# Queries of a cross-attention by seven products over pairs of batches, 256 columns a matmul, on one core

## The chip, the cores and the metric

The kernel runs on one core of a Trainium2 chip, in float32. The metric is the device time of one execution in microseconds; the kernel before took 573.75 us (median of three runs, 572.99 to 574.35).

## The reference

```python
def _L0_xattn_ref(hidden_states, memory_keys, memory_values, attention_mask, Wq, Wout, ln_gamma, ln_beta):
    residual = hidden_states                      # (8, 256, 1024)
    mu = jnp.mean(hidden_states, axis=-1, keepdims=True)
    var = jnp.var(hidden_states, axis=-1, keepdims=True)
    x = (hidden_states - mu) * jax.lax.rsqrt(var + LN_EPS) * ln_gamma + ln_beta
    Q = _split_heads(x @ Wq.T)                    # 32 heads of 32
    K = _split_heads(memory_keys)
    V = _split_heads(memory_values)
    scores = jnp.einsum('bhsd,bhtd->bhst', Q, K) * HEAD_DIM ** (-0.5)
    scores = jnp.where(attention_mask[:, None, None, :], scores, -jnp.inf)
    probs = jax.nn.softmax(scores, axis=-1)
    attn = jnp.einsum('bhst,bhtd->bhsd', probs, V)
    attn = attn.transpose(0, 2, 1, 3).reshape(B, S, HIDDEN)
    return residual + attn @ Wout.T
```

Keys and values are the same array, the context, of 256 rows for each of the 8 batches.

## The kernel before

The work is a software pipeline over 64 steps n. A step is a batch (n // 8) and a group of four heads (n % 8), that is 128 of the 1024 query features. Iteration n of the loop issues, for different steps, everything that is due: the scores of step n+1 on TensorE (`sc`, four PSUM banks, one set only), pieces of the output projection of the batch before (`po`), the values of earlier steps (`pv`), the query matmuls that are due (`pq`, one bank), and then the softmax of step n+1. The softmax goes over all engines: VectorE subtracts and masks (`e<-sc`, with the row minimum `mn` beside it), ScalarE takes the exponential and its sum (`e<-e,mn`), VectorE the reciprocal (`rden`), GpSimd or, for heads listed in the plan, ScalarE normalises (`e<-e,rden`), VectorE transposes in blocks of 32 (`pT<-e`), and DMAs on SP's queue swap the blocks (`pT<-pT`, `pT<-pc`). Since there is one set of four `sc` banks, the scores of the next step wait until VectorE has read all of this one's.

The order within each engine is written by hand: the calls in an iteration, and the table `PLAN`, which says in which iteration each side job is issued. An entry of `wq`, for example, is [iteration, name, quarter, engine]; the numbers under `b2`, `b3`, `rel` (after: `b2`, `b3`, `even`, `odd`) are the iterations of the loads, statistics, normalisations, transposes (`xe<-x`) and block moves (`xnT<-xe`, DMAs) of a batch's x. `qp` names DMAs that go to GpSimd's queue; all others go to SP's.

Side jobs that matter here: the normalisation of x needs `bn_stats`, an `rstd` on GpSimd, a `shift` on GpSimd and one ScalarE instruction for each half of 128 rows. The output projection is done by seven products instead of eight, with sums of `wo` on GpSimd (`wo<-wo`) and sums of the attention output `at`, and its results are added into `r`. `make_q` computes a group's queries plainly, with eight matmuls of 256 columns. For batches from `SPLIT` = 3 on, the queries are computed by seven products too (`query_product`): one batch's two halves of 128 rows are the two block rows, the features the block columns. Each product has 16 matmuls of 128 columns, written into `pq`; sums of weights (`sum_wq`) are made in place of weights that are not needed any more, sums of x (`sum_x`) go into a buffer `sx`, the weights that three of the products take are kept in DRAM and loaded again for each batch into `ring` (`load_ring`), and `copy_product` carries results from PSUM to `qa`. A float32 matmul appears as two records in the trace. Products stand in iterations 8(b-1)+2 to 8(b-1)+8: 18 to 24, 26 to 32, and so on to 50 to 56.

## Time and profile before

| what | value |
|---|---|
| runs | 572.99, 573.75, 574.35 us |
| profiled execution, span from first to last instruction | 572.0 us |
| median of the runs less that span | 1.75 us |
| mean granted TensorE clock | 1.000 |
| TensorE matmul busy | 562.9 us (98%) |
| weight loads, beside the matmuls | 394.6 us (69%) |
| VectorE busy | 466.2 us (81%) |
| ScalarE busy | 450.5 us (79%) |
| GpSimd busy | 399.1 us (70%) |
| DMA, SP's and GpSimd's queue, share of 16 engines | 55.2% and 15.1% |

The profile gives for the profiled execution its span; its own time as a run isn't given beside it. In the timeline a row is start, duration, engine, line, operation, output and inputs, with the number of instructions, and in square brackets the idle time before it and what ended it. In a group row the two numbers behind the bar are the busy time and the mean ns of one instruction. Names are shown without the buffer number, so `sc` is any of the score banks.

### The profile page before, as it was taken

To read this page: it belongs to the slowest core of one execution; us is meant where nothing else is said; L and a number is where in the kernel's file an instruction comes from. 1 tells how busy PE (TensorE), PEld (TensorE's weight loads), DVE (VectorE), ACT (ScalarE), POOL (GpSimd) and SP (SyncE) were. 2 spreads that over 40 slices of the span, in tenths; PEclk is the share of its full clock that TensorE was granted. 3 is DMA by queue.
4 is the path that set the end of the run, shared out by engine and by line. 5 is a ranking of instruction groups with operands and counts; after the bars stand their busy time and mean duration, and the time that the engine had idled before them with its cause. 6 is when DMAs were issued, how large, how long until landed. Compare 5 with 4: busy or idle time off the path is not lost.

```text
span 572.0 us, 20001 instructions
## 1 busy us (share of the span) xinstructions
PE 562.9 (98%) x7162; PEld 394.6 (69%) x7162; DVE 466.2 (81%) x1701; ACT 450.5 (79%) x1527; POOL 399.1 (70%) x643
## 2 busy tenths in 40 slices
PE   8999999999999999999999999999999999999998
PEld 7788775767667677667675777667766777755454
DVE  5988899988878888988788987898877878688833
ACT  3699978888779877888768988789868888879920
POOL 1478978887678895787667774686955875267690
PEclk9999999999999999999999999999999999999999
DMA  8768778576777677877888677767866765547551
GB/s 298 278 174 252 203 206 230 133 205 189 203 235 203 205 207 220 257 210 205 214 249 234 206 201 221 229 200 209 233 189 193 226 182 175 145 136 228 153 167 74
DMA packets 45891, 116.93 MB, mean 204 GB/s; under 512 B 9136, under 2 KB 9904, under 8 KB 45792
## 3 DMA queue, kind: packets, MB, share of 16 engines
q1 hardware_dynamic: 38080, 90.14, 55.2%
q0 software_dynamic: 7424, 25.50, 15.1%
q8 instruction: 57, 0.93, 0.7%
q14 instruction: 42, 0.34, 0.2%
q10 hardware_dynamic: 288, 0.01, 0.0%
HBM read 64.23 MB, written 11.53 MB: 132 GB/s over the span
## 4 chain that ended last, share of the span: by engine, by line
PE 69%; DVE 9%; POOL 8%; ACT 6%; issue 4%; DMA 3%; SPq 0%; DVEq 0%; ACTq 0%; POOLq 0%
PE po_S L930 17%; PE pq_A L615 16%; PE sc L654 8%; PE pv L840 8%; PE po_A L930 8%; PE pq_S L615 6%; POOL e L714 5%; ACT e L698 3%; DVE e L694 3%; PE po_end L997 3%; DVE pT L720 3%; DMA pT<-pT 2%; ACT e L712 1%; PE pq L513 1%; DMA wq<-in_wq_dram 1%
## 5 line engine op out<-in xcount | busy, mean ns | idle before, releaser
L698 ACT ACTIVATE e<-e,mn 128x256 f32<-128x256 f32 x512 | 253.7, 502 | 32.8 <-DVE mn L694 30.2
L714 POOL TENSOR_SCALAR e<-e,rden 128x256 f32<-128x256 f32 x408 | 188.5, 476 | 125.0 <-DVE rden L708 116.8
L720 DVE STREAM_TRANSPOSE pT<-e 128x512 f32<-128x512 f32 x256 | 180.4, 707 | 54.6 <-POOL e L714 23.5
L694 DVE CUSTOM_DVE_ANT_0 e<-sc,mb 128x256 f32<-128x256 f32 x512 | 185.1, 415 | 13.0 <-PE sc L654 12.0
L726 ACT COPY pc<-pT 128x512 f32<-128x512 f32 x128 | 78.8, 617 | 43.7 <-DVE pT L720 28.5
L698 ACT ACTIVATION_READ_ACCUMULATOR e<-e,mn 128x1 f32 x512 | 98.9, 193 | 0.0
L513 PE MATMUL pq<-xnT,wq 128*128 128x256 f32 (+1 forms) x368 | 84.5, 383 | 0.0
L513 PEld LDWEIGHTS pq<-xnT,wq 128*128 128x128 f32 x368 | 68.6, 190 | 14.6 <-issue 3.4
L930 PE MATMUL po_S<-wo,at 128*128 128x512 f32 x152 | 73.5, 606 | 1.0 <-DVE r L972 0.7
L654 PE MATMUL sc<-k,qa 32*128 32x256 f32 x1024 | 73.8, 401 | 0.1
L654 PEld LDWEIGHTS sc<-k,qa 32*128 32x128 f32 x1024 | 45.9, 184 | 39.0 <-issue 17.8
L840 PE MATMUL pv<-pT,v_all 64*32 64x128 f32 x3584 | 61.0, 273 | 1.0 <-ACT e L712 0.6
L840 PEld LDWEIGHTS pv<-pT,v_all 64*32 64x32 f32 x3584 | 51.9, 105 | 12.8 <-issue 7.7
L930 PE MATMUL po_A<-wo,at 128*128 128x512 f32 x128 | 59.3, 604 | 0.1
L930 PE MATMUL po_S<-wo,s 128*128 128x512 f32 x104 | 49.9, 607 | 0.3 <-DVE rden L708 0.3
L708 DVE RECIPROCAL rden<-den 128x2 f32<-128x2 f32 x256 | 37.9, 148 | 13.1 <-ACT e L698 12.1
L712 ACT ACTIVATE e<-e,rden 128x256 f32<-128x256 f32 x104 | 46.8, 500 | 1.0 <-DVE rden L708 1.0
L615 PEld LDWEIGHTS pq_A<-xnT,wq 128*128 128x128 f32 x352 | 41.1, 192 | 5.6 <-issue 4.7
L930 PEld LDWEIGHTS po_S<-wo,at 128*128 128x128 f32 x152 | 26.0, 190 | 25.7 <-issue 23.9
L694 DVE DVE_READ_ACCUMULATOR2_ANT mn<- 128x1 f32 x512 | 42.3, 83 | 0.0
L615 PE MATMUL pq_A<-xnT,wq 128*128 128x128 f32 x352 | 41.2, 275 | 0.3 <-issue 0.3
L930 PEld LDWEIGHTS po_A<-wo,at 128*128 128x128 f32 x128 | 23.0, 189 | 26.5 <-issue 24.4
(116 smaller groups left out, 687.6 us busy)
## 6 DMA issues: line engine op xcount, KB each, us to landing
pT<-pT SPq DMA_DIRECT2D x128, 128.0 KB, 3.4
pT<-pc SPq DMA_DIRECT2D x128, 128.0 KB, 4.0
v_all<-in_kv_dram POOLq DMA_DIRECT2D x17, 512.0 KB, 4.8
k<-in_kv_dram SPq DMA_DIRECT2D x30, 256.0 KB, 4.2
r<-in_x_dram SPq DMA_DIRECT2D x26, 256.0 KB, 4.0
ring<-kept_T SPq DMA_DIRECT2D x11, 512.0 KB, 5.8
xnT<-xe SPq DMA_DIRECT2D x79, 64.0 KB, 3.9
out_dram<-r POOLq DMA_DIRECT2D x18, 256.0 KB, 3.7
```

Source lines behind the costliest of these rows:

```text
L513: nc.tensor.matmul(pqs[n], wq[:, o, c, :], xnTs[b](c), start=(c == 0), stop=(c == NC - 1),)
L615: nc.tensor.matmul(pqs[b][:, o, :], w[:, c], x_[:, c], start=begins and o + c == 0, stop=c == NK - 1, skip_group_check=True,)
L654: nc.tensor.matmul(scs[n][j][:, s, :], qa[r, n % NQ, ts(s, P)], ks[n - n % 2][r, n % 2, :], start=True, stop=True,)
L694: nc.vector.tensor_tensor_reduce(out=e[:, s, :], in0=pss[j][:, s, :], in1=mbs[n // NQ], scale=1.0, scalar=NO_SCORE, op0=ALU.add, op1=ALU.m ...
L698: nc.scalar.activation(e[:, s, :], e[:, s, :], AF.Exp, bias=mn[:, s : s + 1], scale=-1.0, accum_out=den[:, s : s + 1],)
L708: nc.vector.reciprocal(rden, dens[j])
L712: engine.activation(es[j][:, s, :], es[j][:, s, :], AF.Copy, scale=rden[:, s : s + 1])
L714: engine.tensor_scalar(es[j][:, s, :], es[j][:, s, :], rden[:, s : s + 1], 1.0, ALU.mult, ALU.mult,)
L720: nc.vector.transpose(pT[:, :, :, j, :, :].rearrange("p a i s k -> p (a i) s k"), es[j].rearrange("p s (b t) -> p b s t", t=K),)
L726: nc.scalar.copy(pc[:, :, ts(j, 2)], pT[:, 1, :, ts(j, 2)])
L840: nc.tensor.matmul(pvs[n][r][j * HD : (j + 1) * HD], vs[n - n % 2][ts(r, 2 * K), n % 2, i, ts(j, HD)], pT[ts(r, 2 * K), :, i, j, :, :], st ...
L930: nc.tensor.matmul(po, operand(b, name)[:, c], wo[:, which, c], start=begins and c == 0, stop=c == NK - 1, skip_group_check=not begins,)
```

## The change

Two batches at a time, (2,3), (4,5) and (6,7), become the two block rows of the seven products, so `SPLIT` is 2 and batch 2 is included. A product is done in two halves of two 128-feature groups, each with 8 matmuls of 256 columns (all rows of one batch); there are 14 half products for a pair, in iterations 8b-6 to 8b+7 for even b: 10 to 23, 26 to 39 and 42 to 55. The sums of x are written in place over `xnT` (24 GpSimd instructions instead of 20). The odd batch's queries lie in `qlo` and `qhi` (the latter in the first half of `ring`), from which `scores` reads them. ScalarE copies three of the products with 36 instructions of 256 columns (before 80 of 128), VectorE adds the others with 24 instructions (before 15), and GpSimd adds `qlo` to `qhi` after P6 (`after`). The sums of weights take other places and other forms, all on GpSimd, at iterations 7 to 20 (before, 3 of 16 on VectorE, 11 to 22). Weights B11, B21, T1 and half of T3 are kept and loaded again in 14 loads (before 26). The preparation of x is rescheduled in pairs: batch 3's loads move to iterations 5 and 6, its statistics to 7 and 8, its normalisations to 8 and 9 and both transposes to 9. The plan of the output projection (`aside`, `p1late`) now treats batches 0, 2 and 4 in one way and the others in the other. The entries of `qp` for `ring` and most `mv` DMAs are gone, so that these are issued on SP's queue: GpSimd's DMA instructions fall from 75 to 53.

```diff
-PLAN = {'wq': [[14, 'T1', 3, 'V'], [17, 'T3', 0, 'P'], [11, 'T1', 0, 'P'], ...
+PLAN = {'wq': [[7, 'T1', 0, 'P'], [7, 'T1', 1, 'P'], [10, 'T2', 0, 'P'], ...
...
- 'b3': {'loads': [-13, -11],
-        'stats': [-10, -9],
-        'norms': [-9, -8],
-        'trans': [-8, -6],
+ 'b3': {'loads': [5, 6],
+        'stats': [7, 8],
+        'norms': [8, 9],
+        'trans': [9, 9],
...
- 'SPLIT': 3,
- 'rings': [[-3, -3], [0, 0], [2, 2]],
+ 'SPLIT': 2,
+ 'rings': {'B11': [-8, -6], 'B21': [-7, -5], 'T1': [-4, -2], 'T3': [None, 1]},
...
+ 'aside': [0, 2, 4],
...
- 'p1late': [0, 3, 2, 4, 5],
+ 'p1late': [0, 2, 4],
...
+    PRODUCTS_Q = (
+        ("P1", 0), ("P2", 0), ("P1", 1), ("P2", 1), ("P5", 0), ("P6", 0), ("P3", 0),
+        ("P5", 1), ("P6", 1), ("P3", 1), ("P7", 0), ("P4", 0), ("P7", 1), ("P4", 1),
+    )
+    FACTORS = {
+        "P1": ("A11", "B11"), "P2": ("A12", "B21"), "P3": ("S4", "B22"), "P4": ("A22", "T4"),
+        "P5": ("S1", "T1"), "P6": ("S2", "T2"), "P7": ("S3", "T3"),
+    }
...
     def query_product(b, p):
-        name, which, begins = Q_PRODUCTS[p]
...
-            pqs[b] = ps_q.tile([P, NK, P], F32, tag="pq", name=f"pq_{b}_{name}")
...
-        for o in range(NK):
-            w = weights(which, o)
+        name, half = PRODUCTS_Q[p]
+        begins = name not in ("P2", "P4")
+            pqs[b] = ps_q.tile([P, 2, S], F32, tag="pq", name=f"pq_{b}_{name}")
+        x_, w_ = FACTORS[name]
+        x_, w = x_part(b, x_), weights_of(b, w_, half)
+        for o in range(2):
             for c in range(NK):
                 nc.tensor.matmul(
-                    pqs[b][:, o, :], w[:, c], x_[:, c], start=begins and o + c == 0,
-                    stop=c == NK - 1, skip_group_check=True,
+                    pqs[b][:, o, :], w[:, o, c], x_[:, :, c].rearrange("p a s k -> p s a k"),
+                    start=begins and o + c == 0, stop=c == NK - 1, skip_group_check=True,
                 )
...
+        to, of = {
+            "P6": (qlo, qlo), "P3": (c12, qhi), "P7": (qhi, qhi), "P4": (qlo, qlo),
+        }[name]
+        nc.vector.tensor_tensor(to if name == "P3" else to[:, two], pqs[b], of[:, two], ALU.add)
+        if name == "P6":
+            after.append(partial(nc.gpsimd.tensor_tensor, qhi[:, two], qhi[:, two], qlo[:, two], ALU.add))
...
+    def query(n):
+
+        b, o = divmod(n, NQ)
+        if b < 2 or b % 2 == 0:
+            return qa[:, o]
+        return qlo[:, o] if o < NK else qhi[:, o - NK]
...
-    firsts = {NQ * (b - 1) + 2: b for b in range(SPLIT, B)}
-    products = {n + p: (b, p) for n, b in firsts.items() for p in range(len(Q_PRODUCTS))}
+    PAIRED = range(SPLIT, B, 2)
+    products = {NQ * b - 6 + p: (b, p) for b in PAIRED for p in range(len(PRODUCTS_Q))}
```

Three places show how the instructions stand. The first is GpSimd between the normalisation of step 8 (`e_2`, `e_3`) and that of step 9 (`e_0` behind it), first before, then after:

```order
L714 TENSOR_SCALAR e_2_1299<-e_2_1299,rden_2_1323 128x256 x2
L714 TENSOR_SCALAR e_3_1310<-e_3_1310,rden_3_1329 128x256 x2
L534 TENSOR_TENSOR wq<-wq,gs 128x1024
L350 TENSOR_TENSOR wo<-wo 128x512
L714 TENSOR_SCALAR e_0_1418<-e_0_1418,rden_0_1441 128x256 x2
```

The names in the rows after are the same, with other buffer numbers.

```order
L709 TENSOR_SCALAR e_2_1301<-e_2_1301,rden_2_1329 128x256 x2
L709 TENSOR_SCALAR e_3_1312<-e_3_1312,rden_3_1336 128x256 x2
L394 TENSOR_TENSOR rstd_1325<-ve_0_1341,mhalf 128x1
L515 TENSOR_TENSOR wq<-wq,gs 128x1024
L337 TENSOR_TENSOR wo<-wo 128x512
L560 TENSOR_TENSOR ring<-wq 128x512 x2
L709 TENSOR_SCALAR e_0_1430<-e_0_1430,rden_0_1453 128x256 x2
```

An `rstd` of batch 3 and two sums T1 (`ring<-wq`) have come in ahead of step 9's normalisation.

The second is VectorE between the block transposes of step 10 and the first read of step 11's scores (`e_0<-sc_0`), before:

```order
L708 RECIPROCAL rden_3_1593<-den_3_1575 128x2
L720 STREAM_TRANSPOSE pT_1544<-e_2_1562 128x8x64
L720 STREAM_TRANSPOSE pT_1544<-e_3_1573 128x8x64
L399 BN_STATS st_1_1609<-x_1158 128x6 x2
L402 BN_AGGR mv_1456<-st_1_1609 128x2
L404 TENSOR_SCALAR ve_1_1613<-mv_1456 128x1
L694 ISA e_0_1645,mn_0_1646<-sc_0_1622,mb_1215 128x256
```

And after, where `xe` is the transposed x of batch 3:

```order
L703 RECIPROCAL rden_3_1608<-den_3_1590 128x2
L715 STREAM_TRANSPOSE pT_1559<-e_2_1577 128x8x64
L715 STREAM_TRANSPOSE pT_1559<-e_3_1588 128x8x64
L471 STREAM_TRANSPOSE xe_1627<-x_1159 128x32x32 x2
L689 ISA e_0_1661,mn_0_1662<-sc_0_1638,mb_1216 128x256
```

The statistics of the second half of x_3 went to an earlier step, and both transposes of x_3 came to this one, behind ScalarE's normalisation of that half.

The third is TensorE between the scores of step 25 (the first two rows) and those of step 26 (the last two), before:

```order
L654 MATMUL sc_2_3507<-k_3040,qa 128x256
L654 MATMUL sc_3_3508<-k_3040,qa 128x256
L930 MATMUL po_S_3320<-wo,at_1_2329 128x512 x2
L615 MATMUL pq_A_3519<-xnT_1963,wq 128x128 x16
L654 MATMUL sc_0_3601<-k_3310,qa 128x256
L654 MATMUL sc_1_3602<-k_3310,qa 128x256
```

And after, where the queries of batch 3 come from `qlo`:

```order
L649 MATMUL sc_2_3473<-k_3031,qlo 128x256
L649 MATMUL sc_3_3474<-k_3031,qlo 128x256
L925 MATMUL po_S_3306<-wo,at_1_2359 128x512 x2
L649 MATMUL sc_0_3552<-k_3291,qlo 128x256
L649 MATMUL sc_1_3553<-k_3291,qlo 128x256
```

The query product between the two is gone; the two `po` matmuls stay.

More of the change, by code (lines that the diff above doesn't have):

```diff
@@ L158 @@
  'vtail': 56,
+ 'vo': [4, 5, 6, 7],
  'again': [58, 59],
@@ L1317, in xattn_kernel @@
                 sum_at(b, "S2", slice(0, NK - 1))
-        for slot, name in ((n + 2, "S1"), (n + 2, "S2"), (n + 1, "S4"), (n - 1, "S3")):
-            if slot in firsts:
-                sum_x(firsts[slot], name)
+        while after:
+            after.pop(0)()
+        for one, name in x_sums[n]:
+            for part in range(2):
+                sum_x(one, name, part)
         if b == B - 2:
```

232 lines of the change are left out of this document (95 added, 137 removed), and 10 rows, old and new, of the table PLAN.

## The prediction

> **What bounds the kernel now.** I read the page's shares first, then its chain, then the waits of TensorE, and after these the timeline at the places where the change moves work.
>
> ```profile
> span 572.0 us, 20001 instructions
> PE 562.9 (98%) x7162; PEld 394.6 (69%) x7162; DVE 466.2 (81%) x1701; ACT 450.5 (79%) x1527; POOL 399.1 (70%) x643
> PE 69%; DVE 9%; POOL 8%; ACT 6%; issue 4%; DMA 3%; SPq 0%; DVEq 0%; ACTq 0%; POOLq 0%
> PE busy L246 <- POOL ring masks.py:199: 1.4, 1, 1.4
> PE po_S L930 <- DVE r L972: 0.7, 1, 0.7
> ```
>
> TensorE is busy for 98% of the span, and the chain runs over it for 69%. The list of its waits (total, times, longest) has nothing above 1.4 us, and none of its larger entries is `sc`. So TensorE's own work counts in full, and whatever makes TensorE wait counts in full too. The second can happen often: the scores of step n+1 go into the same four banks as those of step n, so `sc` may start only when VectorE has read the last of the old ones (`e<-sc`). Where TensorE's step is short, this is close. The profiled execution has a span of 572.0 us against a median of 573.75 us; I work on the span and add the 1.75 us that lie between.
>
> **Part 1: TensorE's work, -7.7 us.** A product of 128 columns and a plain query matmul of 256 columns, each with four `po` matmul records before it and `sc` behind it:
>
> ```profile
> 132.49 1.98 PE L930 MATMUL po_S<-wo,at 128*128 128x512 f32 x4
> 134.31 3.62 PE L513 MATMUL pq<-xnT,wq 128*128 128x256 f32 x16
> 137.86 1.15 PE L654 MATMUL sc<-k,qa 32*128 32x256 f32 x16
> ...
> 221.70 1.15 PE L654 MATMUL sc<-k,qa 32*128 32x256 f32 x16
> 222.78 1.98 PE L930 MATMUL po_S<-wo,at 128*128 128x512 f32 x4
> 224.60 3.73 PE L615 MATMUL pq_A<-xnT,wq 128*128 128x128 f32 x32
> 228.26 1.15 PE L654 MATMUL sc<-k,qa 32*128 32x256 f32 x16
> ```
>
> From start to start, 32 records of 128 columns take 228.26 - 224.60 = 3.66 us, and 16 of 256 columns 137.86 - 134.31 = 3.55; from the first `po` it is 5.48 against 5.37. I take 0.12 us less for each slot. Before, the queries are 24 plain groups and 35 products, 59 slots; after, they are 16 groups and 42 half products, 58 slots. Were a half product as fast as a plain group, the saving is 35 x 0.12 + 3.5 = 7.7 us. It could be smaller: another plain group takes as long as a product.
>
> ```profile
> 100.49 3.72 PE L513 MATMUL pq<-xnT,wq 128*128 128x256 f32 x16
> 104.14 1.15 PE L654 MATMUL sc<-k,qa 32*128 32x256 f32 x16
> ```
>
> Here it is 104.14 - 100.49 = 3.65 us, so the gain for each product lies between 0.01 and 0.12, and the whole between 3.9 and 7.7. I take the upper end, since its two sides stand between the same neighbours. The Trainium skill (TensorE: Matmul & The Clock Gate, Back-to-back issue gap) gives an isolated matmul N columns at the clock plus a fixed 2.5 ns; by it alone 16 records fewer are worth 0.04 us a product, and the whole would be an estimated 4.9 us instead of 7.7, between the two rows' answers.
>
> **Part 2: the preparation of batch 3 and the sums T1 at steps 8 to 12, +5.3 us.** Both now come early. GpSimd before:
>
> ```profile
> 87.64 1.85 POOL L714 TENSOR_SCALAR e<-e,rden 128x256 f32<-128x256 f32 x4
> ...
> 91.94 0.56 POOL L407 TENSOR_TENSOR rstd<-ve,mhalf 128x1 f32<-128x1 f32 x1
> ...
> 98.83 1.28 POOL L906 TENSOR_TENSOR s<-at,at 128x512 f32<-128x512 f32 x1
> 100.08 0.27 POOL L417 TENSOR_SCALAR shift<-mv,rstd 128x1 f32<-128x1 f32 x1
> ...
> L564 POOL TENSOR_TENSOR ring<-wq 128x512 f32<-128x512 f32 x3 | 3.9, 1287 | 0.0
> ```
>
> In front of the normalisation of e(9), which begins at 87.64, the queue now holds an `rstd` (0.56) and two sums into `ring` (1.29 each) more: 87.64 + 3.1 = 90.8. VectorE's block transposes of e(9) wait for it, and its later reciprocals stand behind those transposes, so the wait is not made up within the step. Then the next two steps of VectorE and ScalarE:
>
> ```profile
> 92.65 0.39 DVE L694 CUSTOM_DVE_ANT_0 e<-sc,mb 128x256 f32<-128x256 f32 x1
> ...
> 98.90 0.71 DVE L720 STREAM_TRANSPOSE pT<-e 128x512 f32<-128x512 f32 x1 [0.27 <-POOL e L714]
> 99.54 1.24 DVE L399 BATCH_NORM_STATS2 st<-x 128x6 f32<-128x512 f32 x2
> 101.13 0.42 DVE L694 CUSTOM_DVE_ANT_0 e<-sc,mb 128x256 f32<-128x256 f32 x1
> ...
> 103.94 0.69 DVE L968 TENSOR_TENSOR r<-po_A,r 128x512 f32<-128x512 f32 x1
> ...
> 100.38 1.24 ACT L420 ACTIVATE x<-x,shift,rstd 128x1024 f32<-128x1024 f32 x1
> L484 DVE STREAM_TRANSPOSE xe<-x 128x1024 f32<-128x1024 f32 x12 | 14.5, 1206 | 0.0
> ```
>
> The first read of step 10 moves from 92.65 to about 95.8. ScalarE's first normalisation of x_3 (1.24) now stands ahead of the exponentials of e(10), which brings its last block transpose about 3.6 us later, 102.5 instead of 98.90. Behind e(10) there was 1.59 us of statistics (99.54 to 101.13). Now a chain stands there: the `at` sum on GpSimd (1.28), `shift` (0.27), ScalarE's second normalisation (1.24), and the second `xe` transpose (1.21), together 4.0 us, so e(11) begins at about 102.5 + 4.0 = 106.5, 5.4 us late. The last read of e(11) was over at 103.94, and `sc` of step 12 came at 104.14: only 0.2 us of cover. So TensorE waits 5.4 - 0.2, say 5.3 with what it saved just before. The bounds are 4.0 and 6.6: one sum of 1.29 less in this chain, because it falls into idle time, or one more.
>
> **Part 3: steps 13 to 18, +0.3 us.** Another two `ring` sums and two sums of x a place stand on GpSimd here (each 1.28). The existing wait of 0.7 behind `r` may vanish in the earlier stop; the short steps, such as the one that ends with the `sc` at 137.86, may add up to 2. I take 0.3, between -0.7 and 2.
>
> **Part 4: the iterations without a query product, 24 and 40: +4.0 and +2.2 us.** Products ran at slots 18 to 24, 26 to 32 and so on; half products run at 10 to 23, 26 to 39 and 42 to 55. Iteration 24 loses its product, and from `sc` of step 25 to that of 26 TensorE has only 228.26 - 221.70 - 3.66 = 2.9 us of work. VectorE stays what it was:
>
> ```profile
> 214.52 0.41 DVE L694 CUSTOM_DVE_ANT_0 e<-sc,mb 128x256 f32<-128x256 f32 x1
> 223.62 0.41 DVE L694 CUSTOM_DVE_ANT_0 e<-sc,mb 128x256 f32<-128x256 f32 x1
> 226.43 0.69 DVE L972 TENSOR_TENSOR r<-po_S,r 128x512 f32<-128x512 f32 x1
> ...
> 362.92 0.69 DVE L972 TENSOR_TENSOR r<-po_S,r 128x512 f32<-128x512 f32 x1
> ...
> 358.93 1.15 PE L654 MATMUL sc<-k,qa 32*128 32x256 f32 x16
> ...
> L564 DVE TENSOR_TENSOR wq<-wq 128x512 f32<-128x512 f32 x2 | 1.3, 664 | 0.0
> L636 DVE TENSOR_TENSOR qa<-pq_A,qa 128x512 f32<-128x512 f32 x10 | 6.5, 652 | 0.0
> ```
>
> The scores of step 25 are read until 226.4. TensorE would be ready at 221.70 + 2.9 = 224.6: a wait of 1.8 us even if VectorE does nothing more than before. It does more. In step 22 it gets statistics (1.59) beside the product's addition, in step 23 statistics in place of a weight sum (1.59 - 0.66, +0.9), in step 24 an `xe` transpose and an addition in place of statistics (1.21 + 0.65 - 1.59, +0.3). Its interval from e(24) at 214.52 to e(25) at 223.62 is 9.10 us; what idle it has there I count on only for the lower end. So e(25) is 1.2 (without step 22) to 2.8 us later, and the wait 3.0 to 4.6; I take 4.0, and 1.8 for the lower end. At iteration 40 the same reading gives 358.93 + 2.9 = 361.8 against 362.9: 1.1 us at least, and by the same additions up to 2.7 with less on GpSimd; I take 2.2. In iteration 56, where the products end too, TensorE still has `pv` and the last batch's `po`, and I count nothing.
>
> **At no cost.** The copies of the products out of PSUM:
>
> ```profile
> L625 ACT ACTIVATE qa<-pq_S,qa 128x128 f32<-128x128 f32 x40 | 11.3, 366 | 0.4 <-PE pq_S L615 0.2
> L522 ACT ACTIVATE qa<-pq,qa 128x256 f32<-128x256 f32 x8 | 3.4, 462 | 0.0
> ```
>
> ScalarE's copies fall from 80 of 128 columns (366 ns) to 36 of 256 (462 ns for this width), VectorE's additions rise from 15 to 24 at 0.65 us, and GpSimd has 12 more additions and 22 DMA issues fewer. Outside the places above each lies beside TensorE; without that cover VectorE's would be 9 x 0.65 = 5.9 us.
>
> **The sum.** -7.7 + 5.3 + 0.3 + 4.0 + 2.2 = +4.1: a span of 576.1 and a time of 577.9 us. A difference under 0.2% (1.15 us) can hardly be told from none.
>
> **The rivals.**
> *The engines beside TensorE catch up* (chance 0.17). If the holds at steps 12, 26 and 42 don't arise, the saving comes through whole: 572.0 - 7.7 + 1.75 = 566 us, faster. For it speaks that every engine but TensorE is idle for about a fifth of the time or more. Against it speak the 0.2 us of cover at 104.14 and the 1.8 us at 224.6, which is there with no work added. It decides if e(9) doesn't stand behind GpSimd and if VectorE reads e(25) before 224.6.
>
> *Only the bare minimum is lost* (0.17). Half of the hold at step 12 (2.6), 1.8 at step 26 and 1.1 at step 42: -7.7 + 5.5 = -2.2, 571.5 us, faster by 0.4%; with the same holds and the smaller saving of 3.9 it would be 575.
>
> *The wider matmul gains nothing* (0.12). The operand of a half product is 32-element blocks of two batches. If it runs like the group at 100.49, the saving is 3.9, and the time 577.9 + 3.8 = 581.7 us. The rows of L615 speak against any cost of the blocks:
>
> ```profile
> L615 PE MATMUL pq_A<-xnT,wq 128*128 128x128 f32 x352 | 41.2, 275 | 0.3 <-issue 0.3
> L615 PE MATMUL pq_A<-sx,wq 128*128 128x128 f32 x160 | 19.2, 277 | 1.0 <-issue 1.0
> ```
>
> From blocks (`xnT`) a record takes 275 ns, from contiguous sums (`sx`) 277.
>
> *The loads of weights come late* (0.10). 22 DMA issues go from GpSimd's queue to SP's, where they stand between the swaps of pT, which wait for transposes.
>
> ```profile
> ring<-kept_T SPq DMA_DIRECT2D x11, 512.0 KB, 5.8
> ```
>
> A load lands 5.8 us after its issue. Each is issued two slots or more ahead; a slot is 572.0 / 64 = 8.9 us on average, so some 12 us are left for the queue, not much over one step. Three late loads of 2 us would make 584 us.
>
> The forecast itself has 0.44. The chances: faster 0.26 (most of the first two), same 0.08 (the second with a smaller saving), slower 0.66. All terms at their lower ends with the full saving give 572.2, all at their upper ends with the smaller saving 585.8; with part of the first rival, the range is 568 to 586 us.
>
> **What would show it.** The span after should have matmul groups of 16 records with 3.55 us from start to start on the query line; a hold on `sc` of about 5 us near 104 us, released by `e` of VectorE, with e(9)'s normalisation starting some 3 us later than 87.64; and holds on `sc` of steps 26 and 42, where no query stands between two scores. If the list of waits has no such entry on `sc`, or the entries sum to less than the saving, I am wrong; if the query groups take 3.65 us, it is the saving that was mis-sized; a wait of query matmuls for DMA would be the fourth rival.

## The result: 612.6 us, slower by 6.5%, and the profile after

| | before | after |
|---|---|---|
| median of the runs | 573.96 us (572.99 to 574.35, 4 runs) | 612.59 us (608.02 to 616.79, 4 runs) |
| ratio, 95% interval | 1 | 1.0649 [1.0577, 1.0720] |
| span of the profiled execution | 572.0 us | 615.0 us |
| mean granted TensorE clock | 1.000 | 0.972 |

The forecast was 577.9 us with a range of 568 to 586: slower, as it came, but with a tenth of the loss (+4.1 us against +38.6 by the medians). The profiled execution is the slowest of the four (616.79 us); its span is 43.0 us longer than before. The ratio is the one on record; the two medians alone give 1.067, inside its interval. The page of after, first the span and TensorE's share, then the granted clock in 40 slices (15.4 us each, tenths):

```profile
span 615.0 us, 18771 instructions
PE 576.2 (94%) x6586; PEld 381.8 (62%) x6586; DVE 465.3 (76%) x1707; ACT 441.0 (72%) x1475; POOL 401.0 (65%) x633
PEclk9999998997799999997999999999799999999999
```

No engine has become the bound: VectorE and GpSimd have about as many microseconds as before, ScalarE 9.5 fewer, and all three smaller shares. TensorE now waits, and in some slices its clock is lower. The list of its waits (total, times, longest), which had nothing above 1.4 us before:

```profile
PE po_S L925 <- POOL wo L337: 6.5, 2, 4.7
PE pq_P L600 <- DMA wq<-kept_B: 5.3, 1, 5.3
PE pv L835 <- DMA pT<-pT: 5.1, 3, 3.0
PE pq_P L600 <- DMA ring<-kept_B: 3.5, 2, 3.1
PE po_S L925 <- DVE r L967: 2.8, 2, 1.8
PE pq_P L600 <- ACT qa L613: 2.4, 1, 2.4
PE sc L649 <- DVE mn L689: 1.4, 2, 0.8
```

It shows several causes and not one, and the hold that I had forecast, `sc` behind VectorE, is the smallest of those shown. To see where the 43 us lie I took, for every step, the time from the first `sc` of a step to the first of the next, and took off the work between them at the rates of undisturbed groups (16 `sc` records 1.08 us, 128 `pv` records 2.04, a `po` record 0.452, a query record 0.216 at 256 columns and 0.112 at 128). What is left is called lost below; 0.05 to 0.1 us of it stand in any step. So the work is an estimate from these rates: it fell by 8.0 us; the lost time rose from 10.9 to 61.8 us, that is by 50.9, and 50.9 - 8.0 = 42.9 is the difference of the spans. By place, after less before:

| steps | lost more, us | forecast, us |
|---|---|---|
| 7 to 9 | 0.3 | 0 |
| 10 to 12 | 5.9 | 5.3 |
| 13 to 18 (15 and 16 alone 13.0) | 12.8 | 0.3 |
| 23 to 28 | 6.2 | 4.0 |
| 29 to 32 (29 alone 6.3) | 6.8 | 0 (a rival's late loads) |
| 38 to 43 | 6.8 | 2.2 |
| 44 to 48 (46 alone 7.5) | 8.6 | 0 (a rival's late loads) |
| 57 | 2.6 | 0 |
| elsewhere | 0.9 | 0 |

About 13 of the 51 us are a lower clock (busy time of TensorE times one less the granted clock, summed over stretches of 15 us); the rest are waits.

**Steps 10 to 12.** The timeline of after: TensorE's `pv`, VectorE's statistic of x_3, and SP's queue ahead of that load.

```profile
94.12 2.08 PE L835 MATMUL pv<-pT,v_all 64*32 64x128 f32 x64 [3.00 <-DMA pT<-pT]
...
91.65 0.69 DVE L386 BATCH_NORM_STATS2 st<-x 128x6 f32<-128x512 f32 x1 [4.21 <-DMA x<-in_x_dram]
...
79.52 4.97 SPq L244 DMA_DIRECT2D xnT<-xe  x6
...
86.44 0.45 SPq L244 DMA_DIRECT2D x<-in_x_dram  x1
```

VectorE stands still for 4.21 us, because the load of x_3 was issued only at 86.44, behind six block moves that take SP's queue 4.97 us to issue. Behind that statistic stand the transposes of e(9), behind these their swaps (`pT<-pT`), and TensorE's `pv` waits for the swaps.

**Steps 15 and 16.** TensorE, then GpSimd, then SP's queue with batch 3's last moves:

```profile
140.93 1.58 PE L925 MATMUL po_S<-wo,at 128*128 128x512 f32 x2 [1.73 <-POOL wo L337]
144.88 5.39 PE L600 MATMUL pq_P<-xnT,ring 128*128 128x256 f32 x16 [2.37 <-ACT qa L613]
160.81 2.08 PE L925 MATMUL po_S<-wo,s 128*128 128x512 f32 x2 [4.74 <-POOL wo L337]
162.68 4.94 PE L600 MATMUL pq_P<-xnT,wq 128*128 128x256 f32 x16
...
133.40 1.28 POOL L589 TENSOR_TENSOR xnT<-xnT 128x512 f32<-128x512 f32 x1 [4.10 <-DMA xnT<-xe]
138.39 2.48 POOL L337 TENSOR_TENSOR wo<-wo 128x512 f32<-128x512 f32 x2
150.62 2.52 POOL L560 TENSOR_TENSOR ring<-wq 128x512 f32<-128x512 f32 x2
156.45 2.49 POOL L589 TENSOR_TENSOR xnT<-xnT 128x512 f32<-128x512 f32 x2
159.50 1.26 POOL L337 TENSOR_TENSOR wo<-wo 128x512 f32<-128x512 f32 x1
...
129.20 3.76 SPq L244 DMA_DIRECT2D xnT<-xe  x6
```

GpSimd waits 4.10 us for batch 3's moves before its first sum of x; its sums of `wo`, which TensorE's projection needs, stand behind. At 159.50 another sum of `wo` stands behind two sums of weights and two of x. A query group that takes 3.62 us elsewhere takes 5.39 and 4.94 here: that is the clock.

**Steps 29 and 46.** SP's queue and the product that waits, at both places:

```profile
266.85 5.70 SPq L244 DMA_DIRECT2D xnT<-xe  x7
275.93 0.38 SPq L244 DMA_DIRECT2D ring<-kept_B  x1
282.30 6.62 PE L600 MATMUL pq_P<-xnT,ring 128*128 128x256 f32 x16 [3.07 <-DMA ring<-kept_B]
...
433.87 0.53 SPq L244 DMA_DIRECT2D wq<-kept_B  x1
440.80 5.89 PE L600 MATMUL pq_P<-xnT,wq 128*128 128x256 f32 x16 [5.26 <-DMA wq<-kept_B]
```

A load of weights is issued at 275.93 behind seven block moves (5.70 us of issuing), a pair of swaps and another load, and the product that takes it starts at 282.30. Then the group takes 6.62 us instead of 3.62. The windows of the trace (from:to, length, busy times, and the third number from the end the granted clock) show why:

```profile
161.00:165.00 4.00, 4.00 (x8) 2.52 (x9) 3.32 (x15) 3.53 (x17) 3.42 (x7) 0.50 0.74 245
282.00:286.00 4.00, 3.70 (x9) 2.98 (x10) 1.42 (x2) 1.43 (x3) 1.18 (x1) 0.50 0.64 162
441.00:444.00 3.00, 3.00 (x8) 2.38 (x9) 0.29 (x1) 0.85 (x2) 1.35 (x2) 0.50 0.94 335
```

After each stop of 3 us or more TensorE runs at half its clock for a while, and the stop is paid again behind itself. In the whole of this execution there are six stretches at 0.50, from 93.68 and 397.46 for 3.41 us, from 141.46, 158.53, 281.41 and 438.42 for 6.83. TensorE is busy in them for 25.8 us, which at half the clock costs 12.9.

### The profile page after: what moved, and what is told of

Its sections match the earlier page's. It is cut to its first block, busy times and chain, and to the rows that moved or that the text cites. A ratio compares the mean times of both kernels' runs of the same rounds, so it can differ in the third digit from the quotient of the medians.

```text
span 615.0 us, 18771 instructions
## 1 busy us (share of the span) xinstructions
PE 576.2 (94%) x6586; PEld 381.8 (62%) x6586; DVE 465.3 (76%) x1707; ACT 441.0 (72%) x1475; POOL 401.0 (65%) x633
## 5 line engine op out<-in xcount | busy, mean ns | idle before, releaser
L600 PE MATMUL pq_P<-xnT,wq 128*128 128x256 f32 x512 | 119.9, 389 | 5.5 <-DMA wq<-kept_B 5.3
L600 PEld LDWEIGHTS pq_P<-xnT,wq 128*128 128x128 f32 x512 | 99.3, 195 | 33.8 <-issue 15.9
L835 PE MATMUL pv<-pT,v_all 64*32 64x128 f32 x3584 | 63.5, 280 | 7.6 <-DMA pT<-pT 5.1
L835 PEld LDWEIGHTS pv<-pT,v_all 64*32 64x32 f32 x3584 | 54.0, 108 | 20.4 <-issue 8.1
L500 PE MATMUL pq<-xnT,wq 128*128 128x256 f32 (+1 forms) x240 | 55.0, 384 | 0.0
L500 PEld LDWEIGHTS pq<-xnT,wq 128*128 128x128 f32 x240 | 44.6, 190 | 8.2 <-issue 1.7
L649 PE MATMUL sc<-k,qa 32*128 32x256 f32 x640 | 47.9, 401 | 0.1
L600 PE MATMUL pq_P<-xnT,ring 128*128 128x256 f32 x160 | 41.4, 417 | 6.8 <-DMA ring<-kept_B 3.5
L703 DVE RECIPROCAL rden<-den 128x2 f32<-128x2 f32 x256 | 37.6, 147 | 13.1 <-ACT e L693 12.2
L649 PEld LDWEIGHTS sc<-k,qa 32*128 32x128 f32 x640 | 29.6, 184 | 25.1 <-issue 17.6
L600 PEld LDWEIGHTS pq_P<-xnT,ring 128*128 128x128 f32 x160 | 33.1, 211 | 17.7 <-issue 5.4
```

What stands on the lines that cost most here:

```text
L500: nc.tensor.matmul(pqs[n], wq[:, o, c, :], xnTs[b](c), start=(c == 0), stop=(c == NC - 1),)
L600: nc.tensor.matmul(pqs[b][:, o, :], w[:, o, c], x_[:, :, c].rearrange("p a s k -> p s a k"), start=begins and o + c == 0, stop=c == NK - 1 ...
L649: nc.tensor.matmul(scs[n][j][:, s, :], query(n)[r, ts(s, P)], ks[n - n % 2][r, n % 2, :], start=True, stop=True,)
L703: nc.vector.reciprocal(rden, dens[j])
L835: nc.tensor.matmul(pvs[n][r][j * HD : (j + 1) * HD], vs[n - n % 2][ts(r, 2 * K), n % 2, i, ts(j, HD)], pT[ts(r, 2 * K), :, i, j, :, :], st ...
```

## The experiments

All kernels but one (the holds in the kernel before) are after with an edit. "Lost" is counted as above, from the profiled execution; ratios are to the kernel before in the same job (1.0649 for after). One execution stands for each version, and what a step loses varies even where an edit changes nothing near it: in the ten versions that keep the late loads of weights as they are in after, itself included, step 29 lost 2.6 to 7.6 us and steps 45 and 46 together 4.5 to 8.8; in the five that leave batch 3 and GpSimd's work up to step 16 alone, steps 15 and 16 lost 13.9 to 15.2. A change that stays within such a spread shows nothing.

### The stop at steps 15 and 16: who is behind?

Theory A: GpSimd's first sum of x is issued ahead of other work, waits for batch 3's moves, and holds GpSimd's queue up. Theory B: GpSimd simply has too much to do there (84.0 us busy in after on steps 7 to 17, 72.2 before). First, the sums of x go behind the sums of weights of their iteration, and the first pair's first one an iteration later:

```diff
-            x_sums[NQ * b + slot].append((b, name))
+            x_sums[NQ * b + (-3 if b == 2 and name == "S1" else slot)].append((b, name))
...
         for one in sums[n]:
             one()
+        for one, name in x_sums[n]:
+            for part in range(2):
+                sum_x(one, name, part)
```

> The changed kernel, with the sums of x issued behind the weight sums in each iteration, and S1 of the first pair one iteration later (13 instead of 12). Theory A: what was lost at steps 15 and 16 (lag 5.6 us at step 15, 18.5 at step 17: 13 us) comes from GpSimd's queue, where S1 of the first pair waits 4.10 and 1.25 us for the moves of batch 3's x, with the sums of wo, that po needs, behind it. Then the waits of po on wo (1.73 and 4.74) and of the query product on qa (2.37) go, TensorE's clock stays at 1.00 there, and the time falls by 10 to 13 us. Theory B: GpSimd simply has too much work in iterations 13 to 15; then the waits only move and the time falls by less than 4 us.

Measured: 606.74 us, 1.0568 [1.0516, 1.0621]. The two steps lose 12.2 instead of 13.9 us. The stop has moved to the product itself, as its largest wait shows:

```profile
PE pq_P L600 <- POOL xnT L589: 10.3, 3, 8.4
```

What followed later gained more (46: 5.4 instead of 7.6; 29: 2.6 instead of 6.3), within the spread of steps that no edit touched. So the place in GpSimd's queue isn't the cause. Next, twelve sums of weights one or two iterations later (B):

```diff
-  [13, 'T1', 2, 'P'], [13, 'T1', 3, 'P'], [14, 'T2', 2, 'P'], [15, 'T2', 3, 'P'], [17, 'T3', 0, 'P'], ...
+  [15, 'T1', 2, 'P'], [15, 'T1', 3, 'P'], [16, 'T2', 2, 'P'], [16, 'T2', 3, 'P'], [18, 'T3', 0, 'P'], ...
```

> The changed kernel, with 12 of the 16 wq sums one or two iterations later (T1 of quarters 2 and 3 at 15, T2 at 16, T3 at 18 and 20, T4 at 19 and 21), nothing else. Theory A (S1 waits for the moves, and all behind it waits too): S1's wait of 5.4 us stays, the sums of wo are still behind it; a gain of 2 to 4 us from the two ring sums (2.5 us) that leave iteration 14. Theory B (too much work on GpSimd in iterations 13 to 15): 5 us of work leave these iterations, the waits on wo go, 8 to 13 us faster.

Measured: 610.49 us, 1.0618 [1.0566, 1.0669]; steps 15 and 16 lose 13.4. Later sums don't help. Nor does it to take GpSimd's normalisations of eight heads of steps 10 to 16 to ScalarE:

```diff
- 'scaled': [[40, 1, 'A'], ...
+ 'scaled': [[10, 3, 'A'], [12, 1, 'A'], [13, 1, 'A'], [14, 0, 'A'], [14, 3, 'A'], [15, 3, 'A'], [16, 1, 'A'], [16, 2, 'A'], [40, 1, 'A'], ...
```

> The changed kernel, with eight more heads of steps 10 to 16 normalised on ScalarE instead of GpSimd (7.6 us of GpSimd's queue in the ten steps where it is busy 84 us). Theory B (GpSimd is too full there): the loss at steps 15 and 16 (14 us) falls by 5 us or more. Theory J (batch 3's x, with its load, statistics, normalisation, transposes and moves, is there too late for the first pair): less than 2.5 us, the stops stay at 15 and 16.

Measured: 611.18 us, 1.063 [1.0555, 1.0705], 12.0 us lost. Theory J: the chain of batch 3 (load, statistics, normalisation, transposes, moves) simply arrives late. Batch 3's moves are freed from it by taking batch 2's x once more, so that batch 3's own queries are left out:

```diff
-  'moves': [9, 9, 9, 9, 10, 10, 10, 10, 10, 10, 11, 11, 11, 11, 11, 11]},
+  'moves': [7, 7, 7, 7, 7, 7, 8, 8, 8, 8, 8, 8, 8, 8, 8, 8]},
...
-            issue(f'mv{pb(b)}{i}', to_move[b][ts(q, K), a], xes[b][ts(a, K), q])
+            issue(f'mv{pb(b)}{i}', to_move[b][ts(q, K), a], xes[2 if b == 3 else b][ts(a, K), q])
```

> The changed kernel, whose moves for batch 3 take the transposed x of batch 2 once more, in iterations 7 and 8, so that the first pair doesn't wait for batch 3's own preparation, which still runs (batch 3's queries are batch 2's; its time is what counts). Theory J: S1's wait for the moves and with it the stop at steps 15 and 16 goes, 10 us or more of the 14. Theory B: the sums still come late, 8 us or more of it stay.

Measured: 616.13 us, 1.0716 [1.0596, 1.0836]. The stop of step 15 is gone (0.1 us lost), but 10.1 are lost in step 11, 4.1 in 12 and 8.2 in 16. The early moves kept the transposed x of batch 2 in use, and VectorE, whose next transposes write into that buffer, waits for them; so the scores wait for VectorE:

```profile
112.79 2.37 DVE L471 STREAM_TRANSPOSE xe<-x 128x1024 f32<-128x1024 f32 x2 [10.14 <-DMA xnT<-xe]
...
115.89 4.20 PE L649 MATMUL sc<-k,qa 32*128 32x256 f32 x16 [9.83 <-DVE mn L689]
```

Both edits in one:

> Both of the last two: moves of batch 3 from batch 2's x at 7 and 8, and eight heads more on ScalarE. If GpSimd's work and batch 3's arrival bind together (each alone gains little), steps 15 and 16 lose 3 us or less here and the time is 12 us or more under the changed kernel's. If the stop stays, it is neither.

Measured: 613.85 us, 1.0677 [1.0592, 1.0762]; 10.5 us lost in step 11, 1.5 in 15, 4.5 in 16. Last, GpSimd's six sums of weights of iterations 10 to 15 are left out, and the moves stay as they are:

```diff
     def sum_wq(to, o, engine=nc.gpsimd):
+        if to == "T2" or (to == "T1" and o > 1):
+            return
```

> The six sums of weights of iterations 10 to 15 (T2, and the second half of T1) are left out, 7.5 us of GpSimd's work (six of 1.25); the products that take them use what lies there instead (the second half of T1 is zero). All else is as after. Theory B (GpSimd holds too much work on steps 10 to 16, and its backlog stops TensorE): of the 13.9 us lost on steps 15 and 16 at most 6.5 are left, the waits of po for wo go, and the time falls by some 7 us, to about 605. Theory J (the x sums wait for batch 3's moves, and GpSimd's queue behind them): the wait of 4.1 us for the moves stays, step 15 still loses about 6, and only step 16 gets better, by the two ring sums that stood ahead (2.5) to 5 us: 608 to 610.

Measured: 608.25 us, 1.0555 [1.0483, 1.0626]. Step 15 loses 7.9 (after 6.9), step 16 loses 4.1 (after 7.0). GpSimd's first sum of x and the sums of `wo` behind it, and TensorE at the two places:

```profile
135.80 2.49 POOL L592 TENSOR_TENSOR xnT<-xnT 128x512 f32<-128x512 f32 x2 [8.77 <-DMA xnT<-xe]
139.47 2.48 POOL L338 TENSOR_TENSOR wo<-wo 128x512 f32<-128x512 f32 x2
...
142.01 1.70 PE L928 MATMUL po_S<-wo,at 128*128 128x512 f32 x2 [2.83 <-DMA pT<-pc]
159.46 2.07 PE L928 MATMUL po_S<-wo,s 128*128 128x512 f32 x2 [2.36 <-POOL wo L338]
```

With less to do GpSimd waits 8.77 us for the moves instead of 4.10, and its sum of x begins no earlier (135.80; after, 133.40): SP's queue issues the last six of these moves from 130.50 to 135.25 here, from 129.20 to 132.96 in after. The row at 142.01 names a swap, but the two sums of `wo` end at 139.47 + 2.48 = 141.95. Step 15 is thus the arrival of batch 3's moves (J): it goes when they are free and stays when GpSimd is. The sums of weights (B) are worth 2.9 us in step 16 and 1.9 over both steps; by the median the run lies 4 us below after, but the two intervals overlap.

### Steps 10 to 12

Theory E, the forecast's: GpSimd's two sums T1 in iteration 7 delay the normalisation of e(9). Theory F: the load of x_3 is issued late. T1 goes from iteration 7 to 10 (and T2 from 10 to 12):

```diff
- [[7, 'T1', 0, 'P'], [7, 'T1', 1, 'P'], [10, 'T2', 0, 'P'], [10, 'T2', 1, 'P'], ...
+ [[10, 'T1', 0, 'P'], [10, 'T1', 1, 'P'], [12, 'T2', 0, 'P'], [12, 'T2', 1, 'P'], ...
```

> The changed kernel, with the sums T1 of quarters 0 and 1 in iteration 10 instead of 7, and T2 of them in 12 instead of 10; nothing else. What is tested is part 2 of the forecast: step 10 lost 4.4 us and step 12 1.5. If it was GpSimd's queue ahead of the normalisation of e(9) (theory E), both shrink, together by 3 us or more. If it is SP's queue and the DMA engines (the wait of 3.00 us of pv for a swap of pT at 94.12; theory F), step 10 keeps its 4.4 us within 0.7.

Measured: 614.5 us, 1.0689 [1.0629, 1.075]; step 10 loses 4.2 instead of 4.4, and steps 15 and 16 lose 16.6. So the two sums alone don't hold step 10. Then (H) x_3's second load an iteration earlier:

```diff
- 'b3': {'loads': [5, 6],
+ 'b3': {'loads': [5, 5],
```

> The changed kernel, with the second load of batch 3's x asked for in iteration 5 instead of 6. Theory H: step 10's 4.4 us come from VectorE, which waits 4.21 us for that load (bn_stats at 91.65, the load issued on SP only at 86.44); then step 10's loss goes, the first pair's moves come some 4 us earlier, and steps 15 and 16 lose less too: 4 to 9 us faster. Rival: the wait for the swap of pT comes back by itself (SP's queue is late, whatever VectorE does): less than 1.5 us.

Measured: 612.54 us, 1.0675 [1.063, 1.072]. Step 10 loses 2.0 instead of 4.4, but 11 and 12 lose 4.5 instead of 2.0, and by step 13 as much is lost as in after (11.3 and 11.4): the next link of the same chain takes over. And the forecast's cause is not out: it stands right behind the load. GpSimd in after, VectorE in this run, and VectorE in the run with T1 later:

```profile
89.62 1.83 POOL L709 TENSOR_SCALAR e<-e,rden 128x256 f32<-128x256 f32 x4
...
90.67 0.71 DVE L715 STREAM_TRANSPOSE pT<-e 128x512 f32<-128x512 f32 x1 [2.55 <-POOL e L709]
...
90.26 0.69 DVE L386 BATCH_NORM_STATS2 st<-x 128x6 f32<-128x512 f32 x1 [2.93 <-DMA x<-in_x_dram]
```

In after the normalisation of e(9) begins at 89.62, 2.0 us later than before (87.64), and VectorE's statistic later still, at 91.65. With the load early, the transposes of e(9) wait 2.55 us for that normalisation; with T1 later it begins at 87.04, and VectorE waits for the load until 90.26. Two holds lie side by side, and each run takes away one; no run takes away both and leaves the rest as in after.

### Late loads of weights

Theory C: the 14 loads stand too far behind in SP's queue. They go to GpSimd's queue:

```diff
+  'ringB110': 1, 'ringB111': 1, 'ringB210': 1, 'ringB211': 1, 'ringT10': 1, 'ringT11': 1, 'ringT31': 1,
```

> The changed kernel, with its 14 reloads of kept weights issued on GpSimd's queue instead of SP's. Theory C: they come late because SP's queue issues them behind the swaps of pT and six or seven block moves of x (0.8 to 0.9 us of queue each); then the waits of the query products for kept_B (3.07, 0.41 and 5.26 us) go, with the half clock behind them, and the time falls by 10 to 13 us. Rival: the transfers themselves are slow (DMA engines 0.9 busy there, 5 to 6 us each) or GpSimd's queue is as late; then less than 4 us, and waits of e on GpSimd's queue appear.

Measured: 616.22 us, 1.0696 [1.0632, 1.076]. Steps 29 and 46 lose 1.3 and 0.5 us instead of 6.3 and 7.6, as C says. But 31, 32, 47 and 48 now lose 13.0 (after 1.7), with waits behind VectorE's additions in place of those for loads:

```profile
PE po_S L926 <- DVE r L968: 8.0, 6, 2.2
```

The loads put at the head of an iteration's DMAs, with the second halves one iteration later:

```diff
- 'rings': {'B11': [-8, -6], 'B21': [-7, -5], 'T1': [-4, -2], 'T3': [None, 1]},
+ 'rings': {'B11': [-8, -5], 'B21': [-7, -4], 'T1': [-3, -1], 'T3': [None, 1]},
...
-        between += rings[n]
+        ahead = rings[n] + ahead
```

> The changed kernel, with the reloads of kept weights still on SP's queue, but at the head of an iteration's DMAs instead of behind the first swaps; the second halves of B11, B21 and T1 and the first of T1 one iteration later (where their buffer is free). Theory C (late in SP's queue): the waits for kept_B at steps 29 and 46 (6.3 and 7.6 us with the clock) go, and no new ones come on GpSimd: 8 to 13 us faster. Rival: the swaps behind the loads come late instead: waits of pv for pT, less than 4 us in all.

Measured: 625.63 us, 1.0928 [1.0844, 1.1013]: 10.3 and 10.0 us lost at 29 and 45. The load that was issued at 275.93 is issued at 282.62, behind six more moves; the expectation missed that the iteration later outweighs the place at its head. It does show that the waits follow the issue:

```profile
PE pq_P L600 <- DMA ring<-kept_B: 15.7, 2, 8.0
...
278.24 4.28 SPq L244 DMA_DIRECT2D xnT<-xe  x6
282.62 0.53 SPq L244 DMA_DIRECT2D ring<-kept_B  x1
```

Then SP's queue is relieved instead (C'), by the 13 block moves that the kernel before had on GpSimd's queue:

```diff
+  'mv3_9': 2, 'mv2_7': 1, 'mv3_2': 2, 'mv7_11': 1, ... 'mv2_11': 1, 'mv3_0': 2,
```

> The changed kernel, with the 13 block moves of x that GpSimd's queue had before put back there (of batches 2, 3 and 7). Theory C': SP's queue as a whole is too full (489 DMA instructions of 0.6 us, moves 0.7), so that taking 13 away gains at steps 8 to 16: 3 to 6 us faster. Rival: it is the order on SP, not its fill, that makes single transfers late: within 2 us of the changed kernel.

Measured: 607.75 us, 1.0611 [1.0585, 1.0637]: steps 45 and 46 lose 0.1 us (after 8.8); step 29 loses 3.2, which is within the spread. And the loads on ScalarE's queue, which holds nothing else of that kind:

```diff
-        issue(f'ring{pb(b)}{name}{half}', weights_of(b, name, half),
+        nc.scalar.dma_start(weights_of(b, name, half),
```

> The changed kernel, with the 14 reloads of kept weights issued from ScalarE's queue at the same place of the program. ScalarE reaches the end of a softmax some 5 us before SP's swaps are through. Theory C (late only because of SP's queue): the losses at steps 29 and 46 (6.3 and 7.6 us) fall to 1 us or less without new ones of that size at 31, 32, 47 and 48, where GpSimd's queue was held by the loads in an earlier run: 8 to 13 us faster. Rival: ScalarE, held by a load whose buffer is not free, passes the wait on: 0 to 4 us.

Measured: 609.95 us, 1.0635 [1.0604, 1.0666]: 29 loses 0.06, 46 1.4, but 30 loses 4.7. On this queue as on GpSimd's the late loads are gone. At the first place much of the gain comes back as another wait within two steps (29 to 32 lose 6.3 us, in after 8.1); at the second most of it stays here (44 to 48 lose 2.5, after 9.0), but not on GpSimd's queue (8.0).

### Iterations 24 and 40, and the clock

Theory D: the iterations without a query product leave too little work over VectorE. The last product goes one iteration later, so that 23 and 39 have none:

```diff
-    products = {NQ * b - 6 + p: (b, p) ...
+    products = {NQ * b - 6 + p + (p == 13 and b < 6): (b, p) ...
```

> The changed kernel, with the last half product of the first two pairs one iteration later (24 and 40, the iterations that have no query product); iterations 23 and 39 have none then. Theory D, the forecast's part 4: sc of steps 26 and 42 no longer waits for VectorE, 4 to 6 us faster. Rival: VectorE stays late, and the hold moves to sc of steps 25 and 41 or to the next steps: less than 2 us.

Measured: 616.99 us, 1.0711 [1.0665, 1.0756]. The hold moves: step 24 loses 5.5 us (after 0.7), step 40 loses 6.4 (1.3), and its waits are

```profile
PE po_S L925 <- DVE r L967: 10.1, 3, 4.4
PE sc L649 <- DVE qlo L621: 3.2, 2, 1.6
```

The gap costs wherever it stands. Theory G: a stop is paid twice, by the half clock behind it. In the kernel before, idle statistics on VectorE hold `sc` up, with nothing else changed:

```diff
+        for _ in range({28: 6, 44: 6, 40: 8, 48: 8, 24: 11, 32: 11}.get(n, 0)):
+            nc.vector.bn_stats(gs[:, :6], wo[:, B22, 0])
```

> The kernel before, with idle work on VectorE (bn_stats of 0.6 us into a free buffer) ahead of the reads of the scores in six iterations: 6 of them (3.7 us) in 28 and 44, 8 (4.9) in 40 and 48, 11 (6.7) in 24 and 32. VectorE's slack there is 1.8 to 3.1 us, so TensorE should be held by about 0.5 to 1, 2.4, and 4.2 to 5 us. Theory G: a hold over some 3 us costs more than its length, because the granted clock falls to a half behind it; the long holds then cost 1.5 to 3 us more than TensorE's own wait, the short ones nothing more; in all about 18 us. Rival: every hold costs its own length: in all about 15 us or less, clock 1.00.

Measured: 603.15 us, 1.0492 [1.0435, 1.0549]; the span is 602.0, 30 us longer, where I had expected some 18. VectorE's hold of iteration 24, TensorE behind it, and the windows there:

```profile
224.56 7.97 DVE L1285 BATCH_NORM_STATS2 gs<-wo 128x6 f32<-128x512 f32 x11
233.26 4.20 PE L654 MATMUL sc<-k,qa 32*128 32x256 f32 x16 [4.01 <-DVE mn L694]
237.39 3.67 PE L840 MATMUL pv<-pT,v_all 64*32 64x128 f32 x128
...
228.00:233.00 5.00, 1.26 (x12) 1.06 (x10) 4.79 (x10) 0.04 (x1) 0.00 (x0) 1.00 0.81 203
233.00:238.00 5.00, 4.74 (x40) 2.94 (x48) 4.44 (x22) 4.14 (x17) 2.82 (x7) 0.63 0.67 237
238.00:241.00 3.00, 3.00 (x121) 2.62 (x104) 2.94 (x10) 2.22 (x5) 2.48 (x2) 0.50 0.02 5
```

8.0 us of VectorE's time, of which 1.75 had cover (the time before from VectorE's last read of the scores to the next `sc`), should cost 6.2; from the `sc` before the hold to the second behind it, it cost 8.7. The second long hold had 2.5 us of cover and 0.7 of idle time on VectorE, should cost 4.7 by the same working, and cost 7.5. I put the difference of 2.5 and 2.8 us down to the clock: `pv` alone takes 3.67 instead of 2.11 us, 1.6 more. The rest lies in the scores, which VectorE's reads stretch at the same time, so it isn't separated. The statistics took 0.72 us each, not the 0.6 that I had set in the expectation, so the holds were longer than planned. The Trainium skill (TensorE: Matmul & The Clock Gate, What's actually happening) says that the clock is either full or half, half after an idle window of about 3.4 us and full again after as long a busy one. The rows agree: a stop of 4.01 us, then 0.50 until about 241 us, with 0.63 in the window in which it changes and 0.99 in the next (241 to 247). The stretches of 3.41 and 6.83 us in after fit one and two such windows, but stops of 3.00 and 3.07 us, shorter than one, were enough there.

### Putting things together

All edits that had helped or were thought to (A's, B's and E's edits, the loads ahead, and the first pair's products from the fifth on one iteration later):

> The changed kernel with all of it together: T1 and T2 later as in k5, reloads ahead as in k7, weight sums later as in k2, sums of x behind the weight sums as in k1, and for the first pair all half products from the fifth on, and its sums of x, one iteration later (so that the moves of batch 3 have landed; iteration 24 has a query product then, 14 has none). If the losses at steps 15 and 16 (13 us), 29 and 46 (14 us) and 26 (2 us) are each of these causes, 20 to 30 us faster than the changed kernel, 583 to 592 us; if each comes back at another place, 605 or more.

Measured: 629.48 us, 1.0951 [1.091, 1.0993], with 10.8 and 12.2 us lost at 29 and 45. The span is 13.0 us longer than after's, and 8 of these stand at 29 to 32 and 44 to 48, where the loads ahead act; steps 16 and 17 still lose 14.6. With the x sums later, x_3 early and the loads on ScalarE's queue:

> The changed kernel, with x_3's load early (k9), the reloads on ScalarE's queue (k11) and the sums of x behind the weight sums, with S1 of the first pair at 13 (k1). If the three causes add up: 4 + 4 at steps 10 to 17, 10 at 29 and 46, 2 to 4 elsewhere: 590 to 597 us. If they don't add, 602 or more.

Measured: 607.34 us, 1.0601 [1.0555, 1.0647], no better than the first of the three alone. Theory I: it is the first pair, begun at iteration 10, for which there is no room. Batches 2 and 3 are computed plainly; two pairs are left, the sums of weights come 16 iterations later, and batch 3 is prepared as in the kernel before:

```diff
-    SPLIT = 2
+    SPLIT = 4
...
- PLAN = {'wq': [[7, 'T1', 0, 'P'], ...
+ PLAN = {'wq': [[23, 'T1', 0, 'P'], ...
```

> The changed kernel without its first pair: batches 2 and 3 get plain queries (256 columns, one group an iteration, to iteration 25), the pairs are (4,5) and (6,7), and the sums of weights and their keeping come 16 iterations later; batch 3 is prepared as in the kernel before, batch 5 one or two iterations later than in the changed one. TensorE has 2 groups more than after (60 instead of 58: +7 us). Theory I: what was lost at steps 7 to 17 (19 us beyond the kernel before) and at 23 to 30 (11 us) comes from starting the first pair at iteration 10, where batch 3 must be ready 8 iterations earlier while GpSimd still has the sums of wo: 72 of 91 us busy before, 84 after on the same steps. Then 590 to 600 us, with no loss before step 26. Rival: the products' reloads and sums cost the same wherever they start: the losses move by 16 steps, 610 us or more.

Measured: 603.65 us, 1.0537 [1.0475, 1.06]. Up to step 22 nothing is lost beyond the kernel before (5.2 us in all; after 25.8, before 6.7). From step 26 on 32 us are lost, as many as in after: the pair that now begins first pays at its own beginning, with 5.0 us lost at 31 and again at 39, and waits on

```profile
PE pq_P L616 <- POOL xnT L605: 4.3, 2, 3.0
```

TensorE's work is 6.9 us more than after's. The same, with the loads on ScalarE's queue and the 13 moves on GpSimd's:

> The kernel without the first pair, with the reloads of kept weights on ScalarE's queue and 13 block moves on GpSimd's as in the kernel before. If the reloads of the last pair and the moves are what SP's queue makes late, 6 to 10 us faster than without these two (the loss of 9 us at steps 45 and 46 and some 2 at others): 582 to 590 us. Rival: under 3 us.

Measured: 599.52 us, 1.0453 [1.0412, 1.0494], the best of all, and still slower than the kernel before. No version was found that keeps the products in pairs and is faster than before.

## Why the prediction was wrong

**Part 1 was right.** Forecast -7.7 us; by the rates above the work fell by 8.0. The query groups start to start:

```profile
172.17 3.62 PE L600 MATMUL pq_P<-xnT,wq 128*128 128x256 f32 x16
175.71 1.15 PE L649 MATMUL sc<-k,qa 32*128 32x256 f32 x16
```

175.71 - 172.17 = 3.54 us against the 3.55 that I took. Between two `po` groups, where most products stand, it is 3.57 us for 32 records of 128 columns (20 of 22 places before) and 3.45 for 16 of 256 (23 of 26 after): 0.12 less again. So the rival that the wider matmul gains nothing is out; its row of 3.65 us stood behind `sc`, the product behind `po`.

**Part 2: the size was right, the cause only half, and the place partly luck.** 5.9 us against 5.3. VectorE's times came close to the forecast: its first reads of e(10) and e(11) are at 95.95 and 107.33, forecast 95.8 and 106.5. But the forecast let the transposes of e(9) wait for GpSimd's normalisation alone. That normalisation did come 2.0 us late, and through T1 (it begins at 89.62 with the two sums ahead, at 87.04 without them); but what ended last was x_3's load. I had counted batch 3's statistics as work and did not ask when their data lands: the change takes them forward in the program, and the load stands behind six moves. Nor did TensorE lose the time where I had put it, in one hold of `sc` near 104 us: 3.00 us were `pv` at 94.12, which waits for the swaps of e(9), with half the clock behind it, and the `sc` at 108.38 was stretched to 3.01 us.

**Part 3 is the step that failed most: +0.3 us forecast, 12.8 measured**, outside its bounds of -0.7 and 2. I priced the added sums as work that finds idle time, and without six of them only 1.9 us of steps 15 and 16 went. What I left out is that a sum waits for its operand. The first sum of x needs batch 3's moves, which the change puts into iterations 9 to 11, on SP's queue between swaps; the last six are issued from 129.20 to 132.96, and the sum begins at 133.40. GpSimd's instructions run in program order, and everything behind that sum waited too. With the moves freed, step 15 lost 0.1 us. In step 16 the added sums themselves are part of it: without six of them it lost 4.1 instead of 7.0. In Part 2 I had followed what stands behind a late instruction on VectorE; I did not do it for GpSimd here.

**Part 4 was right in kind and too small**, 6.2 and 6.8 us against 4.0 and 2.2. The two `sc` behind VectorE:

```profile
246.24 2.51 PE L649 MATMUL sc<-k,qlo 32*128 32x256 f32 x16 [0.59 <-DVE mn L689]
...
394.23 3.25 PE L649 MATMUL sc<-k,qlo 32*128 32x256 f32 x16 [0.77 <-DVE mn L689]
```

I had written that `sc` may start only when VectorE has read the last of the old scores. A wait of 0.59 us ahead of the group isn't all: the group itself is stretched from 1.15 to 2.51, since each bank comes free on its own (in the run with idle holds `sc` begins at 233.26, and VectorE's last read of the old scores ends at 235.33). So `sc` of 26 lost 1.9 us and that of 42 lost 2.9, against 4.0 (lower bound 1.8) and 2.2. Most of the rest is waits for VectorE's additions `r` in the steps around (2.8 in the list of waits) and the clock (0.58 between 397 and 400).

**The rival of the late loads came true, and on top.** It had a chance of 0.10 and three late loads of 2 us. There were two long ones, of 3.07 and 5.26 us, and with the clock behind them steps 29 and 44 to 48 lost 14.9 us more. That they are late through SP's queue is shown by the runs with another queue. The forecast had taken two slots or more between issue and use for some 12 us of room; the load issued at 275.93 came 3.3 us before TensorE was ready for it (282.30 - 3.07 = 279.23). I had treated the rivals as ways that exclude each other; this one adds to the forecast, so the upper end of the range should have held both.

**"I count nothing" for iteration 56** was wrong by 2.6 us at step 57.

**No term for the clock.** The prediction priced each stop once. About 13 us came behind the stops; the run with idle holds shows the mechanism without any of the change's other effects.

What stays open: which schedule would let the pairs pay. Most runs moved single waits, and the time fell by 13 us at most. How much of the losses at 23 to 28 and 38 to 43 is each of VectorE's additions wasn't tried.

## What to carry to other kernels

Price an added instruction on an in-order engine by when its operand arrives and by what stands behind it, not by its own duration. Count, for a queue that gets more DMAs, the microseconds that issuing takes ahead of each urgent load. In a kernel whose main engine is 98% busy, small rivals on different queues add up, and a stop of TensorE of 3 us or more is paid again behind itself: the six stretches at half the clock cost 1.5 to 3.0 us each here.

## What the runs showed of the hardware that I had not expected

- After each stop of TensorE of 3 us or more in after (3.00, 3.07, 4.74, 5.26) the granted clock was 0.50, for 3.41 or 6.83 us: a query group of 3.62 us took 6.62 after the wait of 3.07, and 5.89 after that of 5.26. Shorter waits were followed by it too: 1.73 and 2.37 us close together, and 0.77 ahead of scores that were stretched to 3.25. In the kernel before with idle holds the two long holds cost 2.5 and 2.8 us more than their length.
- Issuing block moves costs SP's queue time that looks like nothing on the page: six took 4.97 us at 79.52 and 3.76 at 129.20, seven 5.70. A load of 0.45 us behind them was late by that.
- Less work on GpSimd didn't let its waiting sum begin earlier: the wait for the moves grew from 4.10 to 8.77 us.
